# Neighbourhood loads of an involution kernel: one run of 3584 bytes per partition, or four of 896

## The chip, the cores and the metric

The kernel runs on one core of a Trainium2 chip. The metric is the time of one execution on the device, in microseconds. Before the change it is 2516.47 us, the median of three runs (2514.35 to 2524.09). The profile is of one more execution, with a span of 2517.8 us.

## The reference

The input x has 8 images of 256 channels, 56 by 56 points, in 32-bit floats. Two layers follow each other, each added to its own input. The first is an involution: a convolution of 7 by 7 whose weights differ from point to point and are themselves computed from the normalized input. Cut to what matters:

```python
# layer 0; xn = group norm of x, 32 groups
ker = einsum('bchw,oc->bohw', xn, w_reduce) + b_reduce       # 256 -> 64 channels
ker = einsum('bchw,oc->bohw', ker, w_span) + b_span          # 64 -> 16 groups of 49
patches = stack of xp[:, :, i:i+56, j:j+56] for i, j in 7x7  # xp: xn padded by 3
x = x + (ker * patches).sum over the 49 places               # 16 channels share one ker
# layer 1; xn = group norm of x
out1 = relu(batch_norm(tri_conv(xn, w1)))                    # 3x3, weights -1, 0, 1
out2 = batch_norm(tri_conv(out1, w2))
x = x + relu(out1 + out2)
```

## The kernel before

The program has four parts, one after the other. The involution runs to about 1355 us, the two convolutions from 1376 to 1804 us and from 1837 to 2265 us, and a last pass over all images ends the program. Only the involution is touched.

**Quarters and tiles.** The 256 channels of an image are cut in four quarters of 64 channels (`NCQ` = 4, `CH` = 64). A quarter fills the 128 partitions with its upper half image in the first 64 and its lower half image in the others. A half image, 28 rows of 56 points, is cut in tiles of 3 by 8 points: 10 tile rows (`TY`), 7 tile columns (`TX`); the last tile row has one row of points only. With the margin of 3 points a tile has a neighbourhood of 9 by 14 points, 126 (`NQ`).

**What TensorE does with it.** For each tile and each group of 16 channels, the 7 by 7 weights of its 24 points are written out as a matrix of 126 neighbourhood points by 24 points; `generate` makes these matrices for the quarter to come (matmuls at L627, copies out at L631 and L636). `apply_row` (L646) then multiplies, for one tile row of a quarter: 7 tile columns, 2 halves and 2 pairs of groups make 28 matmuls per row in the program, which the trace counts as 56. The stationary operand is a block of `q`, 126 neighbourhood points by 32 channels (one pair of groups). `pick_out` (L666) takes of each product the half that belongs to the channel's own group and adds it to x.

**Where q comes from.** `prep` (L542) normalizes a strip of 7 rows on GpSimd (xn, L565), turns it with TensorE so that points lie on partitions (pt, L571: 98 points by 7 tile columns by 128 channels), copies it to SBUF with ScalarE (stg, L574), and stores it in DRAM with `store` (L549, L556): in `xt_d` each row has all points (image row, place in the row of a neighbourhood) and in it 7 tile columns of 128 channels, 3584 bytes. The first and last strip of a quarter are stored once more, for the half that borders on the other (the edge store: 42 points, 7 tile columns, 64 channels, in runs of 256 bytes). `load_q` (L592, L597) reads for a tile row its 126 points of 3584 bytes each, one run per partition, into one of four buffers (`NQB`).

**What sets the order.** The text is written out row by row: 40 rows of an image (4 quarters of 10). In each row stand, in this order, a load of the next image or a store of the last quarter, up to two stores of strips (`transfer(2)`), the matmuls of the row, and the load of q four rows ahead (`prefetch`). Then come the statistics, `pick_out`, one or two steps of `generate`, and one step of `prep`. `pin` (L709) holds every engine to this order. All these transfers are issued by SyncE on one queue (q1 in the profile); it waits in order, for a free q buffer (the matmuls of four rows before), and for stg to be copied. The instruction stream of the program is itself moved by the same 16 DMA engines, in queues of its own.

Of the kernel before, what the change touches and what calls it, by code (L numbers as in the profile page):

```python
# [7 lines left out]
F32 = mybir.dt.float32  # L8
# [7 lines left out]
P = 128  # L16
# [3 lines left out]
K, PAD, G = 7, 3, 16  # L20
# [6 lines left out]
CH = P // 2  # L27
NCQ = C // CH
GQ = G // NCQ
GP = GQ // 2  # L30
HH = H // 2
NHW = HH * W

PY, PX = 3, 8
TY, TX = 10, W // PX
# [3 lines left out]
QY, QX = PY + K - 1, PX + K - 1  # L39
NQ = QY * QX  # L40
# [4 lines left out]

HQ = TY * PY + K - 1
RP = TX * P
SR = HH // 4
NSP = SR * QX

# [24 lines left out]
def involution_tri_block_kernel(  # L75
# [3 lines left out]
    nc = tc.nc  # L79
# [7 lines left out]
    def scratch(name):  # L87
# [4 lines left out]
    wq_d = [dram.tile([P, WT * CT * 3 * C], F32, tag=f"wqd{i}", name=f"wqd{i}") for i in range(2)]  # L92
    xt_d = [[dram.tile([HQ * QX, RP], F32, tag=f"xtd{i}_{c}", name=f"xtd{i}_{c}")
             for c in range(NCQ)] for i in range(2)]
# [337 lines left out]
    with ExitStack() as ph1:  # L432
# [6 lines left out]
        def ps_flat(name):  # L439
            return ps_tile(name).rearrange("p a f -> p (a f)")  # L440
# [3 lines left out]
        work = ph1.enter_context(tc.tile_pool(name="work", bufs=2))  # L444
# [41 lines left out]
        def fixed(shape, name, src=None):  # L486
            t_ = fix.tile(shape, F32, tag=name, name=name)
            if src is not None:
                nc.scalar.dma_start(t_, src)
            return t_  # L490
# [11 lines left out]

        xn = fixed([P, TX, SR, QX], "xn")
        nc.gpsimd.memset(xn, 0.0)
        zero = xn.rearrange("p k r x -> p (k r x)")

        for d in (d for ds in xt_d for d in ds):
            for r0, n in ((0, PAD), (PAD + HH, HQ - PAD - HH)):
                e = n * QX * RP // P
                nc.sync.dma_start(  # L510
                    bass.AP(d[:].tensor, d[:].offset + r0 * QX * RP, [[e, P], [1, e]]), zero[:, :e])

# [29 lines left out]
        def prep(b):  # L542

            for c in range(NCQ):
                d = xt_d[b % 2][c][:]

                def store(src, row, o=None, d=d):  # L549

                    n = src.shape[0]
                    if o is None:
                        src, to = src.rearrange("p k c -> p (k c)"), [[1, RP]]
                    else:
                        to = [[P, TX], [1, CH]]
                    nc.sync.dma_start(  # L556
                        bass.AP(d.tensor, d.offset + row * QX * RP + (o or 0), [[RP, n]] + to), src)

                for s in range(HH // SR):
                    xv = xs[b, c][:, s * SR * W:(s + 1) * SR * W].rearrange(  # L560
                        "p (r k j) -> p k r j", k=TX, j=PX)
                    for k, (x0, j0, n) in enumerate(PLACES):
                        to, fr = ((slice(0, TX), slice(0, TX)), (slice(1, TX), slice(0, TX - 1)),
                                  (slice(0, TX - 1), slice(1, TX)))[k]
                        nc.gpsimd.tensor_scalar(  # L565
                            xn[:, to, :, x0:x0 + n], xv[:, fr, :, j0:j0 + n],
                            prm[b][:, c, 0:1], prm[b][:, c, 1:2], ALU.mult, ALU.add)
                    yield
                    pt = ps_flat(f"pt_{b}_{c}_{s}")
                    for k in range(TX):  # L570
                        nc.tensor.transpose(pt[:NSP, k * P:(k + 1) * P],  # L571
                                            xn[:, k].rearrange("p r x -> p (r x)"), ident_sb)
                    stg = work.tile([P, TX, P], F32, tag="stg", name=f"stg_{b}_{c}_{s}")
                    nc.scalar.copy(stg[:NSP].rearrange("p k c -> p (k c)"), pt[:NSP, :RP])  # L574
                    tasks.append(lambda stg=stg, s=s: store(stg[:NSP], PAD + s * SR))

                    e = PAD * QX
                    if s == 0:
                        tasks.append(lambda stg=stg: store(stg[:e, :, CH:], PAD + HH, 0))
                    elif s == HH // SR - 1:  # L580
                        tasks.append(lambda stg=stg: store(stg[NSP - e:NSP, :, :CH], 0, CH))
                    yield


        tasks = []
# [5 lines left out]

        def load_q(b, c, ty):  # L592

            q = qpool.tile([P, TX, P], F32, tag="q", name=f"q_{b}_{c}_{ty}")
            d = xt_d[b % 2][c][:]
            src = bass.AP(d.tensor, d.offset + PY * ty * QX * RP, [[RP, NQ], [1, RP]])
            nc.sync.dma_start(q[:NQ].rearrange("p k c -> p (k c)"), src)  # L597
            return q

        def views(a):  # L600

            n = NT * GQ * NP
            return (a[:NQ, :n].rearrange("q (t f) -> q t f", t=NT),
                    a[:NQ, n:].rearrange("q (t f) -> q t f", t=NE))
# [41 lines left out]
        def apply_row(b, c, a, ty):  # L646


            ps = ps_a.tile([P, 512], F32, tag="pa", name=f"pa_{b}_{c}_{ty}")
            q = loads.pop((b, c, ty))  # L650
            whole, rest = views(a)
            if ty < TY - 1:
                av, n, t0, t1 = whole, NP, ty * TX, (TY - 1 + ty) * TX
            else:
                av, n, t0, t1 = rest, PX, 0, TX
            for k in range(TX):
                for h, t in enumerate((t0, t1)):
                    for g in range(GP):
                        o = h * CH + g * 32
                        nc.tensor.matmul(ps[o:o + 32, k * 2 * n:(k + 1) * 2 * n],  # L660
                                         q[:NQ, k, o:o + 32],
                                         av[:, t + k, g * 2 * n:(g + 1) * 2 * n],
                                         start=True, stop=True)
            return ps, n
# [17 lines left out]
        def prefetch():  # L682
            if queue:
                k = queue.pop(0)
                loads[k] = load_q(*k)
# [48 lines left out]
        for _ in prep(0):  # L734
            transfer(len(tasks))
# [13 lines left out]
        qpool = ph1.enter_context(tc.tile_pool(name="qpool", bufs=NQB))  # L749
# [12 lines left out]
        for m, (b, c) in enumerate(quarters):  # L762
# [6 lines left out]
            for ty in range(TY):  # L769
                r = c * TY + ty  # L770

                if last is not None and ty in (2, 3):
                    store_x1(*last, ty - 2)
                elif more and r in X_AT:
                    load_x(b + 1, X_AT.index(r) // 2, X_AT.index(r) % 2)
                transfer(2)

                row = apply_row(b, c, a, ty)
                prefetch()

                if more and r >= 20:
                    if r == 20:
                        norm = params(b + 1)
                    next(norm, None)
                if ty == 1 and last is not None:
                    gn2_stats(*last, TY)
                elif ty >= 2:
                    gn2_stats(b, c, ty - 1)
                if more and 4 <= r < 20:
                    gn1_stats(b + 1, (r - 4) // NCB, (r - 4) % NCB)  # L790
                pick_out(b, c, ty, *row)
                for _ in range(PER_ROW[ty]):
                    next(gen, None)
                if more and r == STRIPS_AT:
                    strips = prep(b + 1)
                next(strips, None)
                pin()
# [107 lines left out]
```

## Time and profile before

| stretch, us | what runs | PE busy, us | DMA share | GB/s |
|---|---|---|---|---|
| 230 to 1355 | involution, steady | 912.00 of 1125 | 0.73 | 209 |
| 1376 to 1804 | first convolution | 427.16 of 428 | 0.30 | 114 |
| 1837 to 2265 | second convolution | 426.93 of 428 | 0.29 | 112 |
| 2265 to 2518 | last pass | 0 of 253 | 0.98 | 413 |

In the convolutions TensorE never rests, and the last pass is one of transfers. In the involution no engine is full: TensorE is at 81%, the DMA engines at 73% of their time. How to read the rest: a line of waits names the waiting engine and line, what ended the wait, and the sum in us, the number and the longest. "issue" stands where the trace shows nothing that the engine waited for. The DMA queues are listed with packets, MB and their share of 16 engines' time. The median load of q has 441.0 KB; 320 of them are issued.

### The profile page before, as it was taken

What the parts mean: (1) busy time and instruction counts of PE and PEld (TensorE: products, weight loads), DVE (VectorE), ACT (ScalarE), POOL (GpSimd) and SP (SyncE); (2) the same over time, 40 slices, a digit from 0 to 9 for tenths busy, and PEclk for the clock granted to TensorE, in tenths of its full rate; (3) what the DMA queues carried; (4) which work ended last, traced back from release to release, by engine and by line L of the source; (5) the groups of instructions that cost most, each with busy time, mean ns of one, the idle gap of its engine ahead of it and who ended that gap; (6) DMA issues with size and microseconds to landing.
All of it is one profiled execution on the core that took longest, in us unless ns stands there. A gap on an engine that the chain in (4) does not pass through costs nothing.

```text
span 2517.8 us, 69784 instructions
## 1 busy us (share of the span) xinstructions
PE 1841.1 (73%) x30504; PEld 1709.0 (68%) x30504; DVE 1668.8 (66%) x2554; ACT 1173.1 (47%) x2084; POOL 380.1 (15%) x747
## 2 busy tenths in 40 slices
PE   1524877968788787878884999999689999990000
PEld 1323766867677676767774999999689999990000
DVE  4174656555554555646555999999599999984444
ACT  0211343534434343443543666766466666754343
POOL 0300232322323233232321000000000000000000
PEclk9557998989889898988997999999889999995555
DMA  6327677695867869577766322423332332419998
GB/s 158 100 113 210 189 225 220 193 238 168 241 198 214 211 188 244 175 228 207 219 211 234 131 105 105 157 105 128 143 118 105 135 126 105 152 60 419 428 429 378
DMA packets 123644, 485.45 MB, mean 193 GB/s; under 512 B 33102, under 2 KB 35532, under 8 KB 114636
## 3 DMA queue, kind: packets, MB, share of 16 engines
q1 hardware_dynamic: 117024, 440.03, 53.6%
q10 hardware_dynamic: 6316, 40.97, 4.1%
q8 instruction: 240, 3.93, 0.7%
q14 instruction: 64, 0.52, 0.1%
HBM read 315.76 MB, written 165.18 MB: 191 GB/s over the span
## 4 chain that ended last, share of the span: by engine, by line
PE 65%; DMA 14%; issue 10%; DVE 7%; POOL 2%; ACT 1%; ACTq 0%; SPq 0%; POOLq 0%; DVEq 0%
PE c L385 34%; PE pg L627 15%; PE pa L660 8%; PE pt L571 5%; DMA y1f<-y1d 3%; DMA out_y<-x1f 3%; PE pk L524 3%; DMA x1f<-x1d 2%; DMA q<-xtd 2%; DVE a L636 2%; POOL xn L565 1%; DMA w_w<-in_w 1%; DVE x1f L845 1%; ACT a L631 1%; DMA y1d<-y 1%
## 5 line engine op out<-in xcount | busy, mean ns | idle before, releaser
L385 PE MATMUL c<-pl,wq 128*128 128x392 f32 x4608 | 856.2, 348 | 51.5 <-ACT pl L291 32.3
L385 PEld LDWEIGHTS c<-pl,wq 128*128 128x128 f32 x4608 | 854.2, 189 | 53.3 <-ACT pl L291 33.1
L636 DVE TENSOR_TENSOR a<-pg,bt 126x756 f32<-126x756 f32 (+3 forms) x640 | 393.4, 656 | 311.5 <-ACT a L631 256.2
L627 PE MATMUL pg<-kr,wl 64*126 64x140 f32 (+1 forms) x6144 | 492.0, 308 | 88.6 <-issue 65.4
L627 PEld LDWEIGHTS pg<-kr,wl 64*126 64x126 f32 x6144 | 426.8, 209 | 114.1 <-issue 87.2
L660 PE MATMUL pa<-a,q 126*32 126x48 f32 x17920 | 287.6, 213 | 164.3 <-issue 99.4
L660 PEld LDWEIGHTS pa<-a,q 126*32 126x32 f32 x17920 | 236.4, 116 | 222.9 <-issue 182.8
L631 ACT ACTIVATE a<-pg,bt 126x126 f32<-126x126 f32 x768 | 242.9, 474 | 255.0 <-PE pg L627 254.2
L676 POOL TENSOR_TENSOR x<-x,inv 128x168 f32<-128x168 f32 x320 | 165.6, 517 | 837.7 <-DVE inv L673 828.0
L672 ACT ACTIVATE inv<-pa,half_sb 128x168 f32<-128x168 f32 x320 | 125.7, 393 | 319.7 <-PE pa L660 301.6
L673 DVE SCALAR_TENSOR_TENSOR inv<-pa,half_sb,inv 128x168 f32<-128x168 f32 x320 | 118.7, 371 | 214.8 <-ACT inv L672 213.0
L291 ACT CAST pl<-r 128x812 fp32r<-128x812 f32 x192 | 162.4, 867 | 154.2 <-DVE r L286 137.0
L348 ACT ACTIVATE dummy<-y,nc 128x1568 f32<-128x1568 f32 x128 | 205.3, 1604 | 15.6 <-DVE y L371 14.3
L565 POOL TENSOR_SCALAR xn<-x,gn 128x126 f32<-128x126 f32 (+1 forms) x384 | 204.1, 555 | 37.2 <-PE pt L571 30.6
L292 DVE TENSOR_TENSOR pl<-r,pl 128x812 fp32r<-128x812 f32 x192 | 186.6, 999 | 29.8 <-ACT pl L291 28.7
L574 ACT COPY stg<-pt 98x896 f32<-98x896 f32 x128 | 116.9, 913 | 145.1 <-PE pt L571 90.5
L571 PE MATMUL pt<-ident_sb,xn 128*98 128x128 f32 x896 | 149.1, 309 | 34.0 <-POOL xn L565 23.1
L571 PEld LDWEIGHTS pt<-ident_sb,xn 128*98 128x98 f32 x896 | 106.3, 141 | 65.6 <-POOL xn L565 38.4
L136 DVE BATCH_NORM_STATS2 st<-x 128x6 f32<-128x392 f32 x256 | 137.6, 555 | 16.8 <-DMA x<-in_x 16.3
L272 POOL MEMSET xp<- 128x116 f32 x32 | 6.3, 196 | 816.5 <-DVE a L286 816.4
L826 ACT ACTIVATE xp<-raw,bi_bn,sc_bn 128x392 f32<-128x392 f32 (+1 forms) x128 | 84.8, 720 | 71.6 <-DVE a L286 57.1
L816 ACT ACTIVATE xp<-raw,gn 128x392 f32<-128x392 f32 (+1 forms) x128 | 85.2, 721 | 59.1 <-DVE a L286 51.1
(127 smaller groups left out, 1355.9 us busy)
## 6 DMA issues: line engine op xcount, KB each, us to landing
q<-xtd SPq DMA_DIRECT2D x320, 441.0 KB
xtd<-stg SPq DMA_DIRECT2D x128, 343.0 KB
raw<-x1d SPq DMA_DIRECT2D x32, 812.0 KB
raw<-y1d SPq DMA_DIRECT2D x32, 812.0 KB
x<-in_x SPq DMA_DIRECT2D x64, 392.0 KB
x1d<-x SPq DMA_DIRECT2D x64, 392.0 KB
y1d<-y SPq DMA_DIRECT2D x32, 784.0 KB
y2d<-y SPq DMA_DIRECT2D x32, 784.0 KB
```

Of the source, the lines that this page charges most:

```text
L136: nc.vector.bn_stats(st[:, j, :], xt[:, j * NC:(j + 1) * NC])
L291: nc.scalar.copy(hi, r)
L292: nc.vector.tensor_tensor(lo, r, hi.bitcast(F32), ALU.subtract)
L348: nc.scalar.activation(dummy, y[:, to], f, bias=shift[:, to:to + 1], accum_out=stats[:, to, j, n:n + 1])
L385: nc.tensor.matmul(ps[:, to, :NM], wq[:, k, t, dx, to * P:(to + 1) * P], part[:, t, :, dx:dx + W], start=(c == 0), stop=(c == last))
L565: nc.gpsimd.tensor_scalar(xn[:, to, :, x0:x0 + n], xv[:, fr, :, j0:j0 + n], prm[b][:, c, 0:1], prm[b][:, c, 1:2], ALU.mult, ALU.add)
L571: nc.tensor.transpose(pt[:NSP, k * P:(k + 1) * P], xn[:, k].rearrange("p r x -> p (r x)"), ident_sb)
L627: nc.tensor.matmul(dst, wl[rows, c, gp, o:o + NQ], kr[py][rows, px, :], start=True, stop=True)
L631: nc.scalar.activation(whole[:, g0 + i, p0 + j], ps[:NQ, i, j * nt:(j + 1) * nt], AF.Identity, bias=bt[:, c, g0 + i, p0 + j:p0 + j + 1])
L636: nc.vector.tensor_tensor(dst[:, g0:g0 + 2, p0:p0 + nv].rearrange("q g p t -> q g t p"), ps[:NQ, :, t0 * nv:t1 * nv].rearrange("q i (t p) ...
L660: nc.tensor.matmul(ps[o:o + 32, k * 2 * n:(k + 1) * 2 * n], q[:NQ, k, o:o + 32], av[:, t + k, g * 2 * n:(g + 1) * 2 * n], start=True, stop ...
L676: nc.gpsimd.tensor_tensor(xv, xv, iv.rearrange("p t (y x) -> p y t x", x=PX), ALU.add)
```

## The change

The aim is to read the neighbourhoods in runs of 896 bytes. Channels of a strip are ordered anew: where DRAM rows held tile column, then 128 channels, they now hold half and pair of groups (4 of them, `NO`), then tile column, then the 32 channels of the pair (`CP`). So 7 tile columns of one pair are 224 floats, 896 bytes. In SBUF the tile `q` gets 8 floats of room after each of the four parts; with this gap a partition no longer is one run, and a load has 504 runs of 896 bytes for 126 of 3584. The copy to stg does the reordering: it reads as before and writes in pieces of 32 floats. The edge stores, which take one half, become one run of 1792 bytes per point. The matmuls take the same 32 channels from another place of q.

```diff
+NO = 2 * GP
+CP = P // NO
...
-                def store(src, row, o=None, d=d):
+                def store(src, row, o, d=d):
...
-                    if o is None:
-                        src, to = src.rearrange("p k c -> p (k c)"), [[1, RP]]
-                    else:
-                        to = [[P, TX], [1, CH]]
                     nc.sync.dma_start(
-                        bass.AP(d.tensor, d.offset + row * QX * RP + (o or 0), [[RP, n]] + to), src)
+                        bass.AP(d.tensor, d.offset + row * QX * RP + o * TX * CP,
+                                [[RP, n], [1, src.shape[1] * TX * CP]]),
+                        src.rearrange("p o f -> p (o f)"))
...
-                    stg = work.tile([P, TX, P], F32, tag="stg", name=f"stg_{b}_{c}_{s}")
-                    nc.scalar.copy(stg[:NSP].rearrange("p k c -> p (k c)"), pt[:NSP, :RP])
-                    tasks.append(lambda stg=stg, s=s: store(stg[:NSP], PAD + s * SR))
+                    stg = work.tile([P, NO, TX * CP], F32, tag="stg", name=f"stg_{b}_{c}_{s}")
+                    nc.scalar.copy(stg[:NSP].rearrange("p o (k c) -> p k o c", c=CP),
+                                   pt[:NSP, :RP].rearrange("p (k o c) -> p k o c", o=NO, c=CP))
+                    tasks.append(lambda stg=stg, s=s: store(stg[:NSP], PAD + s * SR, 0))
...
-                        tasks.append(lambda stg=stg: store(stg[:e, :, CH:], PAD + HH, 0))
+                        tasks.append(lambda stg=stg: store(stg[:e, GP:], PAD + HH, 0))
...
-            q = qpool.tile([P, TX, P], F32, tag="q", name=f"q_{b}_{c}_{ty}")
+            q = qpool.tile([P, NO, TX * CP + 8], F32, tag="q", name=f"q_{b}_{c}_{ty}")
...
-            src = bass.AP(d.tensor, d.offset + PY * ty * QX * RP, [[RP, NQ], [1, RP]])
-            nc.sync.dma_start(q[:NQ].rearrange("p k c -> p (k c)"), src)
+            nc.sync.dma_start(
+                q[:NQ, :, :TX * CP],
+                bass.AP(d.tensor, d.offset + PY * ty * QX * RP,
+                        [[RP, NQ], [TX * CP, NO], [1, TX * CP]]))
...
-                        o = h * CH + g * 32
-                        nc.tensor.matmul(ps[o:o + 32, k * 2 * n:(k + 1) * 2 * n],
-                                         q[:NQ, k, o:o + 32],
+                        o = h * GP + g
+                        nc.tensor.matmul(ps[o * CP:(o + 1) * CP, k * 2 * n:(k + 1) * 2 * n],
+                                         q[:NQ, o, k * CP:(k + 1) * CP],
```

More of the change, by code (lines that the diff above doesn't have):

```diff
@@ L572, in prep @@
                                             xn[:, k].rearrange("p r x -> p (r x)"), ident_sb)
-                    stg = work.tile([P, TX, P], F32, tag="stg", name=f"stg_{b}_{c}_{s}")
-                    nc.scalar.copy(stg[:NSP].rearrange("p k c -> p (k c)"), pt[:NSP, :RP])
-                    tasks.append(lambda stg=stg, s=s: store(stg[:NSP], PAD + s * SR))
+                    stg = work.tile([P, NO, TX * CP], F32, tag="stg", name=f"stg_{b}_{c}_{s}")
+                    nc.scalar.copy(stg[:NSP].rearrange("p o (k c) -> p k o c", c=CP),
+                                   pt[:NSP, :RP].rearrange("p (k o c) -> p k o c", o=NO, c=CP))
+                    tasks.append(lambda stg=stg, s=s: store(stg[:NSP], PAD + s * SR, 0))
                     e = PAD * QX
                     if s == 0:
-                        tasks.append(lambda stg=stg: store(stg[:e, :, CH:], PAD + HH, 0))
+                        tasks.append(lambda stg=stg: store(stg[:e, GP:], PAD + HH, 0))
                     elif s == HH // SR - 1:
-                        tasks.append(lambda stg=stg: store(stg[NSP - e:NSP, :, :CH], 0, CH))
+                        tasks.append(lambda stg=stg: store(stg[NSP - e:NSP, :GP], 0, GP))
                     yield
```

## The prediction

> **What bounds the kernel now.** I read the chain first, then engine times by stretch, waits, the DMA queues, and last the timeline of TensorE.
>
> The chain, and the stretch from 230 to 1355 us (the involution, all that the change touches), with busy us and instructions of PE, PEld, DVE, ACT and POOL, then clock, DMA share, GB/s:
>
> ```profile
> PE 65%; DMA 14%; issue 10%; DVE 7%; POOL 2%; ACT 1%; ACTq 0%; SPq 0%; POOLq 0%; DVEq 0%
> ...
> 230.00:1355.00 1125.00, 912.00 (x25178) 798.12 (x25174) 622.98 (x1348) 473.62 (x1222) 337.45 (x652) 0.91 0.73 209
> ```
>
> TensorE is busy 912 of 1125 us; VectorE stands at 55%, ScalarE at 42%. So the stage is TensorE's, and the question is what its 213 idle us are. The waits of that stretch:
>
> ```profile
> PE pa L660 <- issue: 98.6, 61, 5.1
> ...
> PE pg L627 <- issue: 61.7, 25, 5.4
> ```
>
> 160 us, in 86 waits of up to 5 us, are "issue": no semaphore that the profile shows ends them. A q that is late is not among the causes there: by the page's waits over the whole run q cost PE 52.9 us in 5 waits, 50.8 of it in one at the start. The queues name the candidate:
>
> ```profile
> q1 hardware_dynamic: 117024, 440.03, 53.6%
> q8 instruction: 240, 3.93, 0.7%
> ```
>
> q8 moved 3.93 MB in 240 packets, 16.4 KB each. PE has 61,008 matmuls and weight loads: 64 bytes apiece are 3.90 MB. So q8 is TensorE's own instruction stream, 256 instructions to a packet. The timeline of PE (start, length, ..., idle before):
>
> ```profile
> 1118.28 0.74 PE L627 MATMUL pg<-kr,wl 64*126 64x140 f32 x8
> 1121.10 0.51 PE L627 MATMUL pg<-kr,wl 64*126 64x140 f32 x4 [2.08 <-issue]
> ...
> 1124.73 0.62 PE L660 MATMUL pa<-a,q 126*32 126x48 f32 x36
> 1128.11 0.45 PE L660 MATMUL pa<-a,q 126*32 126x48 f32 x20 [2.77 <-issue]
> ```
>
> PE stops in the middle of a row of equal matmuls, after every 256 instructions. Set beside the packet records, the q8 packets start at 1118.65 and 1125.29, last 0.93 and 1.26 us, and PE goes on 1.5 us after each ends. Counting instructions through the stage, each such stop lies a whole multiple of 256 from the others and 1.2 to 1.8 us behind a q8 packet's end. They add up to 174 us over 198 packets.
>
> Why is the packet late? TensorE can ask for a block when it enters the block before. From that moment to the packet's start took 2.33 us in the mean. I grouped the 198 waits by what SyncE had issued on q1 and the engines had not yet moved at that moment:
>
> ```
> not yet moved, KB     packets   mean wait us   q1 moved meanwhile, KB
> under 100             40        0.73           28
> 400 to 700            43        1.99           465
> 700 to 1000           34        3.16           798
> 1000 to 1300          20        4.42           1086
> ```
>
> The last column follows the first: the instruction block stands behind whatever was posted before it. This is the lever: TensorE's stops are set by how much of q1 is standing when a block is asked for.
>
> **What the Trainium skill says.** "Runtime: NRT & Kernel Launch", Instruction fetch mechanics: blocks of 16 KiB, 256 instructions, fetched by the sequencer's own DMA queue while it runs the current one. The trace agrees on block and queue; where the page calls crossing a boundary "mostly hidden", the 174 us here say otherwise. "DMA: Bandwidth & Descriptors", Queues, rings and completion order: an engine goes round-robin between queues, at most 64 descriptors of one before the next. The trace shows the block behind up to some 45 descriptors per engine, so neither pure order of arrival nor a limit of 64 is excluded. Same page, Why a DMA increments its semaphore by 16 and not by 1: the engines used are the largest number up to 16 that divides the slowest dimension of both sides. 126 gives 14; the first loads show packets in 14 lanes, 137 ns apart. After the change the DRAM side has 504 rows, the SBUF side 126: again 14.
>
> **The change part by part.**
> - Neighbourhood load (L597), 320 times: 126 packets of 3584 bytes become 504 of 896. No row of 896 is in the trace. 256 bytes took 18 ns, 3584 took 140, 6272 took 239: 8.6 ns + 36.7 ns per KB, so 41.5 ns for 896 and 166 for four. Consecutive packets overlap some 4 ns, giving 152 against 137. The engine pays 11% to 19% more; I take 11%, 1.37 us per load (36 x 38 ns) against 1.23.
> - What SyncE pays to issue it. A load now is issued in 0.31 us when nothing is ahead (0.52 mean). The only transfer with many runs is the edge store, 42 partitions of 7 runs, 294 in all: SyncE held 0.88 us (median) and, alone on the queue at 68.6 us, its 294 packets spread over 0.91 us, 3.1 ns each, though an engine can take one every 14 ns and there are 14. So runs are made at about 3 ns each. For 504 that is 1.5 us; the lower bound is the edge store's 0.88 flat, the upper 504 x 4 = 2.0. At 1.5 us, 312 loads in the stage take 470 us of SyncE against 162; with the other issues (164, of which edge stores fall from 56 to 18) SyncE is issuing for some 595 of 1125 us and no bound. Queued behind it are stores of stg (ScalarE waits for one of its two buffers) and later loads. Loads land 7.2 us (median, 3.0 at the lowest 5%) before their row, which hides one more us.
> - What this does to the standing work. A load was posted in 0.3 us and drained in 1.2, so nearly all of it stood ahead of an instruction block. Posted over 1.5 us and drained in 1.4, a load alone leaves next to nothing standing. Loads are 141 of q1's 231 MB in the stage, 61%. The mean wait of 2.33 us has a floor of 0.73; 1.6 us is standing work. If all that loads contribute went, 60% of it would; since they also mix with transfers that post fast, I take half: 30% less. Each stop is (wait + packet 1.17 + 1.4 us) less the time PE needs for the block (median 4.6 us, 3.2 to 6.9 from the tenth to the ninetieth percentile). Summed block by block this gives 171 us for the 174 measured, and with the part of each wait above 0.8 us scaled: x0.5 63, x0.7 102, x0.8 124, x1.1 197, x1.2 223, x1.3 250 us. So x0.7 saves 72 us. PE busy and stops together make 96% of the stage, so most comes through: 85%, 60 us.
> - Edge stores (L556), 64 times: 294 packets of 256 bytes become 42 of 1792. Engine time 21 x 14 = 300 ns to 3 x 70 = 210, issue 0.88 to 0.31. Worth 0 to 0.3 us of standing work each time; inside the half above.
> - The copy to stg (L574), 128 times 0.905 us, writes runs of 32 elements. No row shows it; between 0 and, at the 1.3 ns per element of the strided kr copies (0.74 us for 560), 0.26 us more: 33 us at most of the 651 that ScalarE idles in the stage. Nothing for the span.
> - Matmuls of L660, number, shape, 32 contiguous weight columns: unchanged. Instruction order on every engine: unchanged.
> - Price: loads come later, and from 1339 us, where no matrices are generated, rows follow every 1.6 to 1.8 us, near the 1.5 us of an issue; DMA also works longer. I put 12 us on this (0 to 40).
>
> Sum: 60 - 12 = 48 us less, 2468 us.
>
> **The rivals.**
> 1. Slower: SyncE posts ahead anyway (runs made faster than 2 ns, or issue not held), and only the longer packets count. Standing work grows by 11% of 61%, and more because queues at a share of 0.73 lengthen faster than their service: waits x1.1 to x1.2. That is 25 to 52 us more than the 171 of the sum, of which 85% is 21 to 44: 2538 to 2560, 2540 taken. For it: issue durations of 0.31 us do not grow with 98 or 126 rows. Against: the edge store's 0.88.
> 2. Much faster: what a block stands behind is a number of descriptors (64 would be 2.4 us of 896-byte packets at most), or the issue is so slow that nothing stands. Waits x0.5 or less: 111 x 0.85 = 94 less, 2420. For it: no wait in the trace passed 45 descriptors. Against: the waits follow bytes closely.
> 3. No difference: slower drain and slower posting cancel, x0.95 to x1: 2510 to 2520.
>
> **How the numbers follow.** The forecast 0.42, rival 1 0.28, rival 2 0.18, rival 3 0.12. Faster by over 0.5%: 0.60; within 0.5%: 0.12; slower: 0.28. Range 2405 to 2550: down to rival 2 with a little more pass-through, up to rival 1 with waits x1.15 and the full price.
>
> **What would show it.** Right: PE's issue waits at L660 and L627 fall to about 100 us; the issues of L597 rise from 0.3 to some 1.5 us; q1 has some 104,800 packets more (320 x 378 less 64 x 252); PE busy unchanged; nothing moves after 1376 us. Wrong: issue of L597 stays at 0.3 and issue waits rise (rival 1); or PE waits for q in many places, because SyncE or the engines can't keep up, which no step above has beyond 40 us.

## The result and the profile after

The kernel became slower: 2535.24 us (median of four runs, 2531.85 to 2538.49) against 2518.82 us (2514.35 to 2524.09) for the kernel before, of which there is one run more than the three above. The ratio is 1.0064, with a 95% interval of 1.0038 to 1.0090, so 16 us were lost where 48 were forecast as gained.

First the stretch from 230 to 1355 us again, in the kernel after (columns as before: PE, PEld, DVE, ACT, POOL busy with instructions, clock, DMA share, GB/s), and PE's waits in it:

```profile
230.00:1355.00 1125.00, 913.55 (x24869) 799.54 (x24869) 618.98 (x1337) 471.24 (x1216) 334.51 (x646) 0.90 0.76 207
```

```profile
PE pa L664 <- issue: 95.6, 58, 5.1
...
PE pg L631 <- issue: 69.4, 25, 7.3
```

In the same 1125 us TensorE got through 309 matmuls fewer; the DMA share rose from 0.73 to 0.76 while the GB/s fell. The two issue waits make 165.0 us where they made 160.3, although the window now holds less of the stage. (Lines have shifted: L660 is now L664, L627 is L631, L597 is L598, and the store of stg, L556, is L554.)

The queues after:

```profile
q1 hardware_dynamic: 221856, 440.03, 55.3%
q8 instruction: 240, 3.93, 0.7%
```

q1 has 104,832 packets more, the number worked out before, for the same bytes; they took 1.7 points more of the 16 engines' time. The instruction queue is as it was. Now SyncE's timeline (start, us, what), a load that had nothing to wait for, first before and then after:

```profile
728.57 0.32 SPq L597 DMA_DIRECT2D q<-xtd  x1
```

```profile
736.76 0.80 SPq L598 DMA_DIRECT2D q<-xtd  x1
```

SyncE is held 0.80 us by such a load (the median over all of them), not 1.5. Where the trace has a load alone on the queue, its first packet started 0.91 us after the issue began in the kernel before and 1.57 us after in the kernel after. So the packets come later, and then they come together: in such loads the first 14 packets start within 0.10 us of each other, where before they took 0.31 us, and from the first packet to the last it is 1.9 us, for 2.0. The standing work at the moment a block of instructions is asked for was 587 KB before and 636 after, in the mean of 200 blocks; single moments scatter so widely that this difference alone shows nothing, but it did not fall.

Nor did SyncE become a bound. Its waits in the stretch, after, still begin with these, waits for a buffer of q to come free and for the copy:

```profile
SPq L598 <- PE pa L664: 278.1, 153, 6.3
...
SPq L554 <- ACT stg L574: 88.8, 27, 7.6
```

Before, the first of them was:

```profile
SPq L597 <- PE pa L660: 338.9, 158, 7.1
```

Another wait for TensorE, put down to L627 before and L631 after, rose from 38.3 to 75.3 us, so the two together fell from 377 to 353 us: SyncE lost 24 us of its slack on these two and keeps most of it.

What the slower stops look like in PE's timeline (start, length, ..., idle before), after:

```profile
1128.49 2.73 PE L631 MATMUL pg<-kr,wl 64*126 64x140 f32 x24
1131.15 1.47 PE L571 MATMUL pt<-ident_sb,xn 128*98 128x128 f32 x7
1132.55 0.62 PE L664 MATMUL pa<-a,q 126*32 126x48 f32 x36
1136.27 0.70 PE L664 MATMUL pa<-a,q 126*32 126x48 f32 x20 [3.10 <-issue]
1136.89 2.07 PE L631 MATMUL pg<-kr,wl 64*126 64x126 f32 x16
```

The stop of 3.10 us is of the kind known from before. But the matmuls beside it are slow as well. Before, equal groups took 1.62 us for 2.73 and 1.15 for 2.07:

```profile
1122.27 1.62 PE L627 MATMUL pg<-kr,wl 64*126 64x140 f32 x24
...
1128.49 1.15 PE L627 MATMUL pg<-kr,wl 64*126 64x126 f32 x16
```

In the trace of after, the granted clock is one half from 1128.8 to 1132.2 us and again from 1135.6 us on. A stop is paid for a second time in slower matmuls.

For what follows I measured the stage from the first to the last matmul of L664. It is 1136.4 us long before and 1152.4 us after; ahead of it lie 215.8 and 216.5 us, behind it 1165.6 and 1167.7. Of the 19 us between the two profiles 16 are in the stage. In it, for every kernel run: the time of q1's data packets (those of four bytes left out), divided by 16 engines; the mean wait from asking for a block to its packet; the sum of PE's stops at blocks; the time at half clock; PE's busy time.

```
kernel            ratio    q1 packets  block wait  stops  half clock  PE busy  stage
                           us          us          us     us          us       us
before            1        808.9       2.32        173.9  214.5       921.8    1136.4
after             1.0064   861.3       2.40        179.5  244.5       931.0    1152.4
e1_order_only     1.0009   799.0       2.21        169.1  224.4       925.0    1135.7
e2_runs_512       1.0123   920.2       2.50        192.1  262.7       938.8    1180.9
e3_runs_1792      1.0054   815.6       2.27        160.4  240.6       929.7    1134.9
e4_tiny           0.9998   800.4       2.22        168.5  213.6       917.3    1128.3
e5_128_lanes16    0.9847   781.7       2.16        148.0  196.3       913.3    1100.9
e6_four_loads     0.9265   331.0       1.11         34.1   78.9       857.3     944.7
e7_128_896        0.9910   836.2       2.21        151.6  217.1       922.0    1114.8
e8_two_dmas       0.9918   801.8       2.12        149.4  178.5       910.0    1103.5
f1_tiny_after     0.9998   802.0       2.31        166.4  228.1       925.5    1132.6
f2_four_dmas      0.9945   838.4       1.74         25.1  156.8       955.7    1112.5
f3_128_two        0.9795   802.3       2.00        126.9  176.0       913.3    1083.9
f4_change_tiny    1.0078   859.1       2.38        180.2  232.0       927.0    1143.3
g1_runs_4096      1.0160   875.6       2.46        192.1  299.4       950.4    1186.9
g2_128_four_6buf  0.9803   871.7       1.61         40.9  198.0       915.0    1095.7
g3_128_1792       0.9850   798.3       2.16        152.1  159.4       900.7    1092.8
```

The ratios are of timed runs; the other columns are of one profiled run each and scatter: before, e1, e4 and f1 differ by nothing that the timing shows, and their stages run from 1128 to 1136 us. Nor is the profiled run always a middling one: that of e2 was 18 us above the kernel's median time, those of e5 and g1 8 and 7 above, those of e3, f4, g3, e8 and f2 8 to 13 below. Single columns of neighbours are therefore not to be set against each other to the microsecond.

### The profile page after: what moved, and what is told of

Read it like the earlier page. It is cut to its first block, busy times and chain, and to the rows that moved or that the text cites. A ratio compares the mean times of both kernels' runs of the same rounds, so it can differ in the third digit from the quotient of the medians.

```text
span 2536.7 us, 69784 instructions
## 1 busy us (share of the span) xinstructions
PE 1852.5 (73%) x30504; PEld 1719.5 (68%) x30504; DVE 1669.2 (66%) x2554; ACT 1173.2 (46%) x2084; POOL 380.1 (15%) x747
## 4 chain that ended last, share of the span: by engine, by line
PE 66%; DMA 13%; issue 10%; DVE 6%; ACT 2%; POOL 2%; ACTq 0%; SPq 0%; POOLq 0%; DVEq 0%
PE c L387 34%; PE pg L631 16%; PE pa L664 9%; PE pt L571 5%; DMA x1f<-x1d 3%; PE pk L526 3%; DMA y1f<-y1d 2%; DMA out_y<-x1f 2%; DVE a L640 2%; POOL xn L565 1%; DMA w_w<-in_w 1%; DMA q<-xtd 1%; DVE x1f L849 1%; ACT a L635 1%; DMA y2f<-y2d 1%
## 5 line engine op out<-in xcount | busy, mean ns | idle before, releaser
L631 PE MATMUL pg<-kr,wl 64*126 64x140 f32 (+1 forms) x6144 | 496.3, 310 | 92.8 <-issue 69.4
L631 PEld LDWEIGHTS pg<-kr,wl 64*126 64x126 f32 x6144 | 429.9, 210 | 118.3 <-issue 90.9
L664 PE MATMUL pa<-a,q 126*32 126x48 f32 x17920 | 292.0, 215 | 171.0 <-issue 102.8
L664 PEld LDWEIGHTS pa<-a,q 126*32 126x32 f32 x17920 | 240.2, 117 | 230.6 <-issue 190.0
```

The source lines that it names most:

```text
L631: nc.tensor.matmul(dst, wl[rows, c, gp, o:o + NQ], kr[py][rows, px, :], start=True, stop=True)
L664: nc.tensor.matmul(ps[o * CP:(o + 1) * CP, k * 2 * n:(k + 1) * 2 * n], q[:NQ, o, k * CP:(k + 1) * CP], av[:, t + k, g * 2 * n:(g + 1) * 2 ...
```

## The experiments

The theories, as the expectations name them. **A**: the loads hold the DMA engines longer, so that blocks of instructions wait longer behind them. **B**: SyncE, held longer by each load, posts other transfers and later loads too late. **C**: the new order, the copy that makes it and the other edge stores cost the time. **T** and **D** came later and are told where they arose.

**Parts of the change, and a larger dose.** e1 keeps the order, the copy and the edge stores and takes the gap out, so that a load is again one run per partition:

```diff
-            q = qpool.tile([P, NO, TX * CP + 8], F32, tag="q", name=f"q_{b}_{c}_{ty}")
+            q = qpool.tile([P, NO, TX * CP], F32, tag="q", name=f"q_{b}_{c}_{ty}")
```

> The new order in DRAM, the reordering copy and the edge stores in one run stay; the gap in q goes, so a load is 126 runs of 3584 bytes again. Theory A (four short packets hold the DMA engines longer, so more stands ahead of the instruction blocks): the loss goes, ratio to the kernel before 0.995 to 1.000, issue waits of TensorE at or a little under 160 us because the edge stores are shorter. Theory B (the issue of a load holds SyncE 0.8 us for 0.3): the same here, since the issue falls back to 0.31. Theory C (the order, the copy or the edge stores cost it): still 1.006.

Measured: 2519.65 us, 1.0009 (0.9992 to 1.0025). A load's issue is back at 0.32 us. C falls: order, copy and edge stores together cost nothing beyond the interval's 0.25%. The copy, which writes in pieces of 32 floats, takes as long as before, 913 ns, as the page of the kernel after has it:

```profile
L574 ACT COPY stg<-pt 98x896 f32<-98x896 f32 x128 | 116.8, 913 | 141.1 <-PE pt L571 92.9
```

e2 is the kernel before with a gap after each tile column, 882 runs of 512 bytes per load:

```diff
-            q = qpool.tile([P, TX, P], F32, tag="q", name=f"q_{b}_{c}_{ty}")
+            q = qpool.tile([P, TX, P + 8], F32, tag="q", name=f"q_{b}_{c}_{ty}")
-            src = bass.AP(d.tensor, d.offset + PY * ty * QX * RP, [[RP, NQ], [1, RP]])
-            nc.sync.dma_start(q[:NQ].rearrange("p k c -> p (k c)"), src)
+            src = bass.AP(d.tensor, d.offset + PY * ty * QX * RP, [[RP, NQ], [P, TX], [1, P]])
+            nc.sync.dma_start(q[:NQ, :, :P], src)
```

> The kernel before, with a gap of 8 floats after each tile column of q: 882 runs of 512 bytes per load, old order, old edge stores. A: a 512-byte packet should take about 27 ns, seven of them 192 for 140, twice the rise of the 896-byte packets: ratio 1.012 to 1.025. B: as the issue time goes; if it is 0.8 us again, 1.006 as with the change. C: 1.000.

Measured: 2546.89 us, 1.0123 (1.0087 to 1.0159). A packet of 512 bytes takes 27 ns in the median and 34 in the mean, so a partition's seven cost 239 ns where a packet of 3584 costs 192 in the mean (strip stores among them, which have the same length); the packets of q1 take 920 us. The issue takes 0.80 us, with 882 runs as with 504: SyncE's hold does not grow with the runs, while the loss doubled. That speaks for A, whose range of 1.012 to 1.025 holds the ratio, and against B.

e3 is the change with one gap in the middle, 252 runs of 1792 bytes:

```diff
-            q = qpool.tile([P, NO, TX * CP + 8], F32, tag="q", name=f"q_{b}_{c}_{ty}")
+            q = qpool.tile([P, 2, 2 * TX * CP + 8], F32, tag="q", name=f"q_{b}_{c}_{ty}")
-                q[:NQ, :, :TX * CP],
+                q[:NQ, :, :2 * TX * CP],
-                        [[RP, NQ], [TX * CP, NO], [1, TX * CP]]))
+                        [[RP, NQ], [2 * TX * CP, 2], [1, 2 * TX * CP]]))
-                                         q[:NQ, o, k * CP:(k + 1) * CP],
+                                         q[:NQ, h, g * TX * CP + k * CP:g * TX * CP + (k + 1) * CP],
```

> The change with q in two parts in place of four: 252 runs of 1792 bytes per load. A: two packets of 74 ns, 148 for 140, a third of the rise: ratio 1.001 to 1.003, or under 1 with the shorter edge stores. B: if the issue of such a load is 0.8 us too, the full loss of the change, 1.006. C: 1.006.

Measured: 2530.44 us, 1.0054 (1.0033 to 1.0075). The issue takes 0.80 us again, two packets 202 ns in the mean, the packets of q1 816 us. The loss is above what A was given, and near that of the change. With e1, e2 and e3 alone, B (0.80 us in all three gapped kernels) was not yet out.

e4 holds SyncE without touching the loads: a transfer of 32 bytes into a tile that nothing reads, ahead of each load of the kernel before.

```diff
+            tiny = qpool.tile([1, 8], F32, tag="tiny", name=f"tiny_{b}_{c}_{ty}")
+            nc.sync.dma_start(tiny, x[b, c:c + 1, 0:8])
```

> The kernel before, and ahead of each load of q one transfer of 32 bytes from x into a tile that nothing reads: SyncE is held about 0.3 us more per load, as good as no bytes more. A: same, 0.998 to 1.002. B: 1.003 to 1.006, as holding SyncE is what costs. C: same.

Measured: 2517.2 us, 0.9998 (0.9976 to 1.0019). SyncE's issuing in the stage grew from 324 to 409 us and its waits for transfers from 41 to 137 us, and no time was lost. The change has SyncE issuing for some 450 us, so this was two thirds of its dose; f2, below, has it issuing for some 815 us and is faster than the kernel before. B falls.

**More and less engine time in the old form.** A load of 126 points is moved by 14 engines, nine points each. e5 loads 128 points (two rows more of xt_d, not used), so that 16 engines take eight each; it is e1 else, one run per partition.

```diff
+    xt_d = [[dram.tile([HQ * QX + 2, RP], F32, tag=f"xtd{i}_{c}", name=f"xtd{i}_{c}")
...
-                q[:NQ, :, :TX * CP],
+                q[:, :, :TX * CP],
...
-                        [[RP, NQ], [TX * CP, NO], [1, TX * CP]]))
+                        [[RP, P], [TX * CP, NO], [1, TX * CP]]))
```

> New order, no gap, and a load brings 128 points in place of 126 (two more than are used): the slowest dimension is then 128, and 16 DMA engines can share it, 8 packets of 3584 bytes each where 14 had 9. Theory A (the time that work stands in the engines ahead of instruction blocks sets the loss): standing work of loads falls by a ninth, ratio 0.990 to 0.997. Theory D (a load whose rows have gaps costs a fixed 6 us or so, whatever its packets): no gap here, so it has no say; without A, 1.000.

Measured: 2479.19 us, 0.9847 (0.9822 to 0.9872), stops of 148 us; a larger gain than A was given. The busiest engine's part of a load fell by a ninth, 11%. That a load now has two engines more shows in q1's packets of four bytes: f2's 960 transfers more bring 14 of them each, and e5, with as many transfers as before, has 12,960 for the 12,320 of the kernels before and after, two more per load.

e6 shows how much hangs on the loads at all: only the first four rows load q, and later rows use these four tiles again.

```diff
+            if len(kept) == NQB:
+                kept.append(kept.pop(0))
+                return kept[-1]
+            q = qpool.tile([P, TX, P], F32, tag=f"q{ty}", bufs=1, name=f"q_{b}_{c}_{ty}")
+            kept.append(q)
```

> The kernel before, with q loaded for the first four tile rows only; all later rows multiply with those four tiles, so the involution's products are of the wrong points. It leaves out 61% of the bytes of the stage. A: issue waits of TensorE fall from 160 us to under 40, ratio 0.93 to 0.95. If instruction blocks did not stand behind loads, the issue waits stay over 120 us and the ratio over 0.98.

It leaves out 316 of 320 loads, so most products are of other points. Measured: 2329.89 us, 0.9265 (0.9239 to 0.9291), a little below A's range. PE's waits from 230 to 1355 us:

```profile
PE pa L666 <- issue: 15.5, 21, 3.1
PE pg L633 <- issue: 15.3, 10, 4.1
```

The instruction queue moves what it moved before, and its blocks are waited for 1.11 us instead of 2.32. This is the ceiling of everything that loads do to this stage: 7.35% of the time. The stage is 192 us shorter: 140 us less of stops and 64 us less of PE's busy time, with some 13 us more of other idling.

e7 puts the four gapped parts of 896 bytes into e5 (its edit as it stands against e5):

```diff
-            q = qpool.tile([P, NO, TX * CP], F32, tag="q", name=f"q_{b}_{c}_{ty}")
+            q = qpool.tile([P, NO, TX * CP + 8], F32, tag="q", name=f"q_{b}_{c}_{ty}")
```

> The change (gaps, runs of 896 bytes) with loads of 128 points on 16 engines: 32 packets of 38 ns per engine, 1.22 us, against 9 of 137 ns, 1.23 us, before. A: ratio 0.998 to 1.002, the loss is gone as an engine holds a load no longer than before. D: 1.003 to 1.006.

Measured: 2494.4 us, 0.991 (0.989 to 0.993), so 0.6% above e5 on the same chip. Both forecasts were too high, since they were made before e5's gain was known; beside e5 the loss is there. Four packets take 211 ns in the mean for 187. The change's loss repeats with another number of engines. An issue takes 0.52 us here, and the loss is the same as at 0.80.

g1 lengthens the engine time without a gap: the order of e1, and runs of 4096 bytes, of which the last 512 are not used. It has the two rows more of xt_d too.

```diff
-            q = qpool.tile([P, NO, TX * CP], F32, tag="q", name=f"q_{b}_{c}_{ty}")
+            qw = qpool.tile([P, RP + P], F32, tag="q", name=f"q_{b}_{c}_{ty}")
+            q = qw[:, :RP].rearrange("p (o f) -> p o f", o=NO)
...
+                qw[:NQ], bass.AP(d.tensor, d.offset + PY * ty * QX * RP, [[RP, NQ], [1, RP + P]]))
```

> New order, no gap; each of the 126 runs of a load is 4096 bytes, 512 of them the start of the next point and not used. One plain transfer per load, issued in 0.31 us, but a packet of about 159 ns for 140: the engines hold a load about as much longer as with four packets of 896. Theory A (time in the engines costs it): 1.004 to 1.008. Theory D (what costs is that one transfer is cut by gaps: held 0.8 us, posted late and in a lump): 0.999 to 1.002.

Measured: 2564.4 us, 1.016 (1.0124 to 1.0196), twice the loss that A was given. A packet takes 227 ns in the mean for 192, the issue 0.32 us as ever. Waits and stops after:

```profile
PE pa L663 <- issue: 94.1, 45, 5.4
PE pg L630 <- issue: 68.8, 26, 6.7
```

The window shows these sums little changed because it holds less of the stage; over the whole stage the stops are 192 us against 169 in e1. Longer time in the engines, here with 14% more bytes per load, is enough for a loss, with one run per partition and a short issue.

**Is it the form?** g3 is e5 with the single gap of e3 (theory **D**: a gapped transfer costs something in itself, whatever its packets):

```diff
-            q = qpool.tile([P, NO, TX * CP], F32, tag="q", name=f"q_{b}_{c}_{ty}")
+            q = qpool.tile([P, 2, 2 * TX * CP + 8], F32, tag="q", name=f"q_{b}_{c}_{ty}")
...
-                q[:, :, :TX * CP],
+                q[:, :, :2 * TX * CP],
...
```

> 128 points on 16 engines, one transfer per load in two parts of 1792 bytes with a gap. Beside 0.985 for 128 points without a gap and 0.991 with three gaps. A: 0.986 to 0.988. D: 0.990 to 0.992, the same as with three gaps.

Measured: 2486.58 us, 0.985 (0.9816 to 0.9884); e5 had 0.9847 on another chip. Two packets take 196 ns in the mean where e5's one takes 187. With 128 points the one gap costs nothing that the intervals of 0.3% show. D's 0.990 to 0.992 lies outside the interval, and e2's loss, twice that of the change in the same form, speaks against a fixed cost too: D falls as a cost of the form itself. Whether the 0.45% that this gap cost in e3 against e1 comes back here, these intervals can't tell.

**The spreading that the prediction wanted.** e8 and f2 post a load in two or four plain transfers in place of one with gaps. f2 moves the very packets of the change (504 of 896 bytes):

```diff
-            q = qpool.tile([P, NO, TX * CP + 8], F32, tag="q", name=f"q_{b}_{c}_{ty}")
+            q = qpool.tile([P, NO, TX * CP], F32, tag="q", name=f"q_{b}_{c}_{ty}")
...
-            nc.sync.dma_start(
-                q[:NQ, :, :TX * CP],
-                bass.AP(d.tensor, d.offset + PY * ty * QX * RP,
-                        [[RP, NQ], [TX * CP, NO], [1, TX * CP]]))
+            for i in range(NO):
+                nc.sync.dma_start(
+                    q[:NQ, i],
+                    bass.AP(d.tensor, d.offset + PY * ty * QX * RP + i * TX * CP,
+                            [[RP, NQ], [1, TX * CP]]))
```

e8 is the same with `range(2)` and halves of 1792 bytes.

> New order, no gap, each load issued as two transfers of 126 runs of 1792 bytes: the packets of the two-part kernel, but each transfer of the plain form that is issued in 0.31 us. A: as the packets, 1.001 to 1.003. D: 1.000, as no transfer has gaps. A loss of 1.005 would say that the packets of 1792 bytes cost more than their length.

> New order, no gap, each load as four plain transfers of 126 runs of 896 bytes: the very packets of the change, issued in 0.31 us apiece, no transfer with gaps. A: 1.004 to 1.008 as with the change. T: SyncE waits far more for older transfers, 0.985 to 0.998; over 1.01 if holding SyncE 1.2 us per load makes q late.

Measured: e8 2496.03 us, 0.9918 (0.9896 to 0.9941); f2 2506.09 us, 0.9945 (0.9923 to 0.9967). No theory had a gain for e8; for f2 T, told below, had one. One load of f2 on SyncE (its four transfers as one line), and PE's waits in f2:

```profile
757.13 1.66 SPq L599 DMA_DIRECT2D q<-xtd  x4
```

```profile
PE pa L665 <- DMA q<-xtd: 83.8, 127, 2.8
...
PE pg L632 <- issue: 11.2, 12, 1.9
...
PE pa L665 <- issue: 9.2, 11, 1.7
```

SyncE posts the four parts over 1.66 us, and the issue waits all but vanish. Four packets take 201 ns in the mean, where the same four of the change take 222. The matmuls pay with 84 us of waiting for q, 127 times up to 2.8 us. With the packets of the change, f2 is 1.2% faster than the change; with the packets of e3, e8 is 1.4% faster than e3. So it isn't the packets alone that decide, but also how the load is cut into transfers.

Was that due to posting, or to the waits for earlier transfers that more transfers bring with them (theory **T**: SyncE, made to wait for earlier transfers, posts less far ahead)? f1 and f4 put the 32 bytes of e4 behind each load of e1 and of the change.

```diff
+            tiny = qpool.tile([1, 8], F32, tag="tiny", name=f"tiny_{b}_{c}_{ty}")
+            nc.sync.dma_start(tiny, x[b, c:c + 1, 0:8])
             return q
```

> New order, no gap, and after each load a transfer of 32 bytes into a tile that nothing reads. Theory T (completion is counted on 8 semaphores in turn, so with more transfers SyncE waits more often until an older one has landed, and less stands in the engines; two transfers per load had 123 us of such waits where one has 40): 0.988 to 0.996, though packets and bytes of loads are those of the kernel before. Theory A (packet time alone): 1.000.

> The change itself, and after each load a transfer of 32 bytes that nothing reads. T: the gain of the waits comes on top of the loss, 0.994 to 1.001. A: 1.006, as with the change.

Measured: f1 2521.53 us, 0.9998 (0.9981 to 1.0015), with 130 us of SyncE's waits for transfers; f4 2539.19 us, 1.0078 (1.0047 to 1.0109). Such waits alone bring nothing, so T falls; f4 confirms the loss of the change on another chip.

**Both gains together.** f3 has the 128 points of e5 and the two plain transfers of e8. g2 has 128 points, the four transfers of f2, and six buffers for four, against the waits for q:

```diff
-NQB = 4
+NQB = 6
```

> 128 points on 16 engines, each load as two plain transfers of 1792-byte runs. If the shorter time in the engines and the waits for older transfers work apart from each other: 0.974 to 0.980. If they are one and the same: 0.984, as with 128 points alone.

> 128 points on 16 engines, each load as four plain transfers of 896-byte runs, six q buffers for four. Four plain transfers took TensorE's issue waits from 170 to 24 us but made it wait 84 us for q. If more buffers let q come in time: 0.960 to 0.975. If SyncE or the waits for older transfers bound it, buffers don't help: 0.980 to 0.990.

Measured: f3 2466.28 us, 0.9795 (0.9765 to 0.9824); g2 2473.28 us, 0.9803 (0.977 to 0.9836). They are level, and lowest of all kernels that do the whole work, though the intervals of e5 and g3 touch theirs; f3 beats the kernel before by 2%. f3 lies where the two gains add, g2 where buffers were said not to help. In g2, from 230 to 1320 us, neither wait is large any more, and others have come up:

```profile
PE pa L665 <- DVE inv L678: 25.8, 9, 4.3
PE pg L632 <- DVE a L641: 23.4, 8, 5.5
PE pt L571 <- POOL xn L565: 22.9, 26, 1.8
PE pa L665 <- DMA q<-xtd: 22.0, 28, 2.7
PE pa L665 <- issue: 21.0, 22, 2.9
```

TensorE now waits for VectorE and GpSimd as well. Against e1 the stops are 128 us less, but the stage less PE's busy time only 30 us (181 for 211): most of what the blocks gave up went to other waits.

## Why the prediction was wrong

The forecast of 2468 us failed by its sign; the first rival, 2540 us, is what came. The range, to 2550, holds the 2535 us by way of that rival alone. Step by step:

- **Blocks of instructions stand behind q1.** Right, and larger than the trace of before could say: without the loads, e6, stops fall from 174 to 34 us and the program by 7.35%. One reading was too wide: PE does not stop after every 256 instructions, but always at a multiple of 256, at some 95 of the stage's 200 blocks.
- **The price of a packet.** Right: 41 ns for 896 bytes against 41.5 estimated. Four packets take 222 ns in the mean of the stage where one of 3584 bytes took 192, 16% more. But the 192 has the strip stores in it. In the kernel after, where their length tells them apart, they took 171 ns; if they did so before, a load's packet took 198 (an estimate from these three means), and the change's four 12% more. Both are inside the 11% to 19%.
- **"What SyncE pays to issue it".** This is the step that failed. From the edge store's 294 runs I made a rate, 3 ns a run and so 1.5 us for 504. The issue took 0.80 us, below even the bound of 0.88, and the same 0.80 for 252, 504 and 882 runs. One row with one number of runs does not tell a rate from a constant, and the range had the constant as its lower bound; the value taken was the rate.
- **"What this does to the standing work".** It fell with it, and by more than the size. The gapped load isn't spread over its issue: its first packet comes 0.66 us later than before (1.57 against 0.91), and the rest as close together. In place of 30% off the waits, they did not fall: 2.32 to 2.40 us in the pair of profiles, and 5% more if the four kernels at the old time (before, e1, e4, f1, from 2.21 to 2.32, mean 2.27) are set against the two with the change (after, f4, mean 2.39), which is hardly more than the four differ. The idea of the step was sound, as f2 shows with the same packets: posted over 1.66 us in four transfers, the stops fall to 25 us. A slip in the sum is small beside this: the 72 us set 102 us computed against 174 measured, and from the 171 computed it is 69.
- **The share that comes through.** The sum had stops only. Between the same groups of four and two profiles the stage grew by 15 us, of which PE idles 8 and is busy 7 us more, though "PE busy unchanged" was a sign of being right. The clock goes with it: over e6, e5, the four at the old time, e2 and g1, half-clock time goes 79, 196, 220, 263, 299 us and busy time 857, 913, 922, 939, 950, about 0.42 us of busy time for each of half clock. The two with the change have 238 and 929, near that line; f2, with 157 and 956, is far above it. The two highest points, e2 and g1, were profiled in runs slower than their median, so the line's slope is rougher than its figures. The step between the two groups alone is no larger than the scatter of single profiles, so it is the row of doses that carries this.
- **Edge stores, copy, instruction order.** Right: e1 measures the three together at 1.0009, with an interval that includes 1.
- **The price of 12 us for late loads.** PE waited 2.1 us for q before and after: nothing. But the term was too small for the case it was made for: in f2, which posts a load over 1.66 us, PE waits 84 us for q, and the gain was 14 us, not 48.
- **Rival 1** had the right end by half the right way: waits grew by some 5%, if at all, rather than 10 to 20%, and PE's longer busy time, which it did not have, made up the difference.

The cause, then: a gapped load keeps the DMA engines busy longer (A), and blocks of instructions, and with them TensorE, wait for it. In the plain form, time in the engines and loss go together: against e1, e5 gains 1.6% with an engine's part of a load 15% shorter, and g1 loses 1.5% with packets 15% longer. That is about 0.1% of the program per 1% of the load's engine time. (These are estimates for loads alone, the strip stores taken out as above: nine packets of 198 ns in e1, eight of 190 in e5, with the 178 ns that stores take in e7; 227 ns a packet in g1.)

**What stays open** is the size. At that rate e3, with 3% more, should lose 0.3% against e1 and lost 0.45%; but the change, with 12% more, should lose 1.2% and lost 0.55% against e1, e7, with 11% more than e5, 1.1% and lost 0.6%, and e2, with 21% more, 2.1% and lost 1.2%. With more than one gap about half of the expected loss came. Either the later first packet of a gapped load gives part back, or the extra bytes of g1 and the two more engines of e5 count by more than the time of a load's packets; no run separates these. How much of e8 and f2 is due to the spread of the posting, and how much to each part being waited for by itself, wasn't separated either. f2's busy time of PE, 30 us above e1's at less time at half clock, is explained in part: the products of the rows (pa) count 345 us as busy where e1 has 292, the matmuls of `generate` (pg) 458 for 476, and with six buffers, in g2, pa has 301. So it goes with the waiting for q; how waiting comes to be counted as busy, no run shows. Holding SyncE longer without any further transfer wasn't tried.

## What to carry to other kernels

If TensorE idles in "issue" at multiples of 256 of its instructions, look at the instruction queue: here a block waited behind what stood on the data queue when it was asked for, and the stage got shorter with less DMA time per load and with loads posted in pieces. A load cut by gaps into more runs was not a load in pieces: it held the engines longer and was posted all at once; plain transfers did what it was meant to do. And a load of 126 partitions was dearer than one of 128: two points more, not used, made the kernel 1.5% faster, with the two transfers 2%.

## What the runs showed of the hardware

- **The clock after a stop.** The granted clock changes in steps of 3.413 us and is 1 or one half. I laid this grid over the stage of before and after. Of windows at full clock with PE idle under 1.5 us, 1 of 433 was followed by half clock; at 1.5 to 2 us 37 of 54; at 2 us or more 50 of 50. From half clock it came back in 85 of 88 cases after a window idle under 0.5 us, and in 3 of 49 after one idle longer. The Trainium skill, "TensorE: Matmul & The Clock Gate", Part 1: The HAM clock gate, has the two states and the window of about 3.4 us, and the trace agrees; it puts the fall after an idle window, and here 2 us of idling in 3.4 were enough. So a stop of 2 us within one such window costs more than 2 us, as the slow matmuls after it show.
- **Issue times.** SyncE's median for a load of 126 partitions was 0.32 us with one run each and 0.80 with two, four or seven; for 128 partitions 0.33 with one and 0.52 with two and four. The edge store fell from 0.88 to 0.38 us with one run per point.
- **A packet, median over the stage**: 512 bytes 27 ns, 896 41, 1792 74, 3584 140, 4096 165; the means lie higher, 34, 56, 101, 192 and 227 ns. Those of 3584 are loads and strip stores together.
